# An order for all five engines worked out before emission, and five places for rows of weights

## The chip, the core and the metric

The kernel runs on one core of one Trainium2 chip. The metric is the device time of one execution in microseconds (us). PE is the matrix engine, DVE the vector engine, ACT the scalar engine, POOL the GpSimd engine, SP the engine whose queue issues most of the DMA transfers. All arithmetic is float32.

## What is computed

```python
# x: (8, 512, 256); Wg, Wu: (8, 256, 1024); Wd: (8, 1024, 256); Sg, Su, Sd: the shared expert's
g = einsum('bsd,edf->ebsf', x, Wg)
u = einsum('bsd,edf->ebsf', x, Wu)
expert_outs = einsum('ebsf,efd->ebsd', silu(g) * u, Wd)
expert_output = einsum('be,ebsd->bsd', gating_probs, expert_outs)
shared = einsum('bsf,fd->bsd', silu(x @ Sg) * (x @ Su), Sd)
out = x + (1 - sg) * expert_output + sg * shared
```

## The kernel before

The eight batch elements are two groups of four, and there are nine experts (the shared one is the ninth). A pair of group and expert is a **unit**; the 18 units run one after the other, named `0_0` to `1_8`. In a unit the four batch elements are combined with four **rows** of weights, a row being 256 columns of gate and up weights (two halves s, gate and up m). By sums and differences of inputs and of weights, prepared on POOL, DVE and ACT, products of several batch elements and rows share matmuls, so that there are fewer of them than in the plain product, and more element-wise work.

A unit is a sequence of 20 **items** (`SEQ`): hubs `h0` to `h3`, one per row (`P_step`, L338, and `Q_step`, L347), and 16 batches. A batch needs a weight difference `u` (`u_form`, L193, POOL), two more differences `w` (`w_form`: ACT multiplies, L203 and L207, then POOL, L210 and L212) and input tiles `v` and `b` that SP loads (L238, L244). In PSUM, ACT copies a sum `Pt` of a hub into a bank (`seed`, L265) and DVE subtracts another (L266); then PE multiplies by `u` and `v` (`R1`, L271), DVE opens a second bank (L281), PE multiplies by `w` and `b` (`R2`, L271), ACT takes silu (L285) and DVE forms the features `h` (L290). The items of the next unit's h0, 0s, h1 and 1s stand between the last batches of a unit (with ' in `SEQ`).

The down product runs along with this, one unit behind: chains `ch` (L454) with weights `ud`, `wd` (`d_forms`, L157 to L164, POOL), and `p`, `q` (L483) on `sums`, to which POOL adds features (L408, or a DMA with accumulation issued by POOL, L418). Partial results `V` go to memory and come back a unit later (L405, L394).

Counted in the code, a unit has 200 matmuls of 256 columns and 52 of 512. PE and POOL keep the order in which the code emits (`manual_schedule`); DVE, ACT and SP get theirs from the Tile scheduler.

The rows of weights lie in `raw`, which has room for four. `load_raw` (L126, four DMAs of 128 KB for a row) overwrites row r with the next unit's row r. It is emitted when the last batch that reads the old row has been formed two items ahead: row 0 with `03b`, row 1 with `13b`, rows 2 and 3 with `23b`. Then `make_at` changes a loaded row in place: ACT multiplies into `at` (L132), and POOL adds (L135). It is emitted two items ahead of its hub. `u` has two places and `w` three.

## Time and profile before

| | us |
|---|---|
| median of 2 runs | 2881.68 (2876.83 to 2886.54) |
| the profiled execution | 2880.3 |
| its span, first to last instruction | 2878.5 |
| PE busy | 2532.1 (88%) |
| DVE, POOL, ACT busy | 2102.2, 2040.5, 1236.2 |
| mean granted clock of PE | 0.947 |

The span is the profiled execution from its first to its last instruction; 1.8 us of the time lie outside it. In a timeline row the columns are start, duration, engine, line, operation, output and inputs, shape, and in brackets the idle time before it and what ended it. The mean of one instruction includes the time in which it overlaps the next one of its engine.

### The profile page before, as it was taken

Reading aid. Unit: us, or ns where it says so; the run is one execution under the profiler, and the core shown is the slowest. Engines: PE = TensorE matmul, PEld = TensorE weight load, DVE = VectorE, ACT = ScalarE, POOL = GpSimd, SP = SyncE. Lnnn points to the kernel's source line nnn. Section 1 sums busy time; section 2 is a strip of 40 time slices with the busy share of each in tenths; the row PEclk is TensorE's granted clock in tenths of the full one; section 3 lists DMA queues with packets and bytes.
Section 4 is the critical chain, followed back from the end, with each engine's and each line's share of the span. In section 5 each row is a group of like instructions: output and inputs, shape, how many; then the busy total and the mean of one; then the engine's idle time right before and its main releaser. Section 6 shows DMA issues by size and latency. Waiting matters only on the chain.

```text
span 2878.5 us, 30400 instructions
## 1 busy us (share of the span) xinstructions
PE 2532.1 (88%) x9112; PEld 1786.0 (62%) x9112; DVE 2102.2 (73%) x3006; ACT 1236.2 (43%) x2586; POOL 2040.5 (71%) x1676
## 2 busy tenths in 40 slices
PE   7789897898888798898987998989899888989897
PEld 5556565565556566666665666656666666666664
DVE  7877786788877676776776666768787676767677
ACT  5444343343434343444434444434344444444442
POOL 6968676685866678595948676767869585959683
PEclk8999998999989999999999999999999999999999
DMA  4476857658665756656465646565755657575646
GB/s 156 125 182 166 231 170 217 190 160 227 195 196 157 196 162 180 173 159 176 134 172 156 180 144 184 154 178 148 191 164 164 182 153 183 154 183 168 172 131 127
DMA packets 325633, 492.28 MB, mean 171 GB/s; under 512 B 73568, under 2 KB 204128, under 8 KB 325472
## 3 DMA queue, kind: packets, MB, share of 16 engines
q1 hardware_dynamic: 295808, 377.05, 41.5%
q0 software_dynamic: 29376, 113.25, 20.8%
q8 instruction: 75, 1.23, 0.2%
q14 instruction: 86, 0.70, 0.1%
q10 hardware_dynamic: 288, 0.04, 0.0%
HBM read 321.43 MB, written 55.57 MB: 131 GB/s over the span
## 4 chain that ended last, share of the span: by engine, by line
PE 47%; POOL 25%; issue 9%; DMA 8%; DVE 6%; ACT 2%; SPq 2%; POOLq 0%; ACTq 0%; DVEq 0%
PE ch L454 11%; POOL sums L408 7%; DMA raw<-in_L_cond_Wu_dram 5%; PE c_23b L271 3%; PE cd L338 3%; PE cd L347 3%; PE c_01a L271 3%; PE c_01b L271 3%; PE c_13b L271 3%; PE p L483 3%; PE c_13a L271 2%; PE q L483 2%; PE c_23a L271 2%; PE c_02b L271 2%; POOL wd L163 2%
## 5 line engine op out<-in xcount | busy, mean ns | idle before, releaser
L454 PE MATMUL ch<-X,ud 128*128 128x512 f32 x432 | 243.4, 648 | 0.0
L408 POOL TENSOR_TENSOR sums<-sums,h_03a 128x1024 f32<-128x1024 f32 x72 | 178.4, 2482 | 72.6 <-DVE h_03a L290 67.0
L193 POOL TENSOR_TENSOR u_01a<-raw 128x512 f32<-128x512 f32 x18 | 23.1, 1282 | 283.8 <-PE c_23b L271 280.8
L132 ACT ACTIVATE at<-raw 128x256 f32<-128x256 f32 x126 | 50.1, 412 | 394.5 <-DMA raw<-in_L_cond_Wu_dram 319.1
L338 PE MATMUL cd<-x,raw 128*128 128x256 f32 x576 | 158.4, 399 | 42.2 <-ACT sg_03b L285 35.1
L408 POOL TENSOR_TENSOR sums<-sums,h_02a 128x1024 f32<-128x1024 f32 x72 | 174.4, 2434 | 5.7 <-DVE h_02a L290 5.7
L347 PEld LDWEIGHTS cd<-x,raw 128*128 128x128 f32 x576 | 117.6, 205 | 91.9 <-issue 72.3
L408 POOL TENSOR_TENSOR sums<-sums,h_01a 128x1024 f32<-128x1024 f32 x72 | 171.3, 2379 | 1.4
L338 PEld LDWEIGHTS cd<-x,raw 128*128 128x128 f32 x576 | 111.5, 198 | 95.9 <-ACT sg_03b L285 48.1
L193 POOL TENSOR_TENSOR u_02b<-raw 128x512 f32<-128x512 f32 x18 | 23.3, 1295 | 206.9 <-PE c_02a L271 206.9
L347 PE MATMUL cd<-x,raw 128*128 128x256 f32 x576 | 157.6, 399 | 7.5 <-ACT Pt L342 7.5
L483 PE MATMUL p<-sums,rawd 128*128 128x512 f32 x288 | 147.9, 597 | 6.8 <-ACT p L480 6.8
L483 PE MATMUL q<-sums,rawd 128*128 128x512 f32 x288 | 148.6, 600 | 3.9 <-DVE accB L374 2.4
L266 DVE TENSOR_TENSOR c_23b<-c_23b,Pt 128x512 f32<-128x512 f32 x36 | 25.1, 698 | 155.2 <-ACT c_23b L265 154.5
L356 ACT COPY Dt<-cd 128x512 f32<-128x512 f32 x144 | 84.0, 584 | 105.7 <-DVE sums L290 104.9
L271 PE MATMUL c_23b<-v_23b,u_23b 128*128 128x256 f32 x144 | 53.7, 510 | 78.1 <-issue 73.4
L342 ACT COPY Pt<-cd 128x512 f32<-128x512 f32 x144 | 83.9, 583 | 65.9 <-PE cd L338 65.8
L271 PE MATMUL c_03b<-v_03b,u_03b 128*128 128x256 f32 x144 | 45.3, 441 | 69.7 <-DVE c_03b L266 43.5
L135 POOL TENSOR_TENSOR raw<-raw,at 128x256 f32<-128x256 f32 (+1 forms) x72 | 97.4, 1353 | 12.9 <-ACT at L132 12.9
L454 PEld LDWEIGHTS ch<-X,ud 128*128 128x128 f32 x432 | 89.4, 207 | 16.0 <-issue 1.9
L376 DVE TENSOR_TENSOR accB<-accB,ch 128x512 f32<-128x512 f32 x104 | 70.8, 681 | 31.8 <-PE ch L454 31.2
L374 DVE TENSOR_TENSOR accB<-ch,accB 128x512 f32<-128x512 f32 x116 | 79.2, 684 | 19.6 <-PE ch L454 19.5
(426 smaller groups left out, 8049.6 us busy)
## 6 DMA issues: line engine op xcount, KB each, us to landing
sums<-h_12a POOLq DMA_DIRECT2D x36, 1024.0 KB, 11.2
sums<-h_13a POOLq DMA_DIRECT2D x36, 1024.0 KB, 10.9
sums<-h_23a POOLq DMA_DIRECT2D x36, 1024.0 KB, 10.5
x<-xd SPq DMA_DIRECT2D x64, 512.0 KB, 3.8
Vd<-V SPq DMA_DIRECT2D x96, 256.0 KB, 2.0
V<-Vd SPq DMA_DIRECT2D x96, 256.0 KB, 3.1
raw<-in_L_cond_Wg_dram SPq DMA_DIRECT2D x128, 128.0 KB, 6.6
raw<-in_L_cond_Wu_dram SPq DMA_DIRECT2D x128, 128.0 KB, 5.7
```

What stands on the lines that cost most here:

```text
L135: gp.tensor_tensor(A, A, tmp[:, s0:], ALU.add)
L163: gp.tensor_tensor(W[:, 0], U, a[0], ALU.subtract)
L271: pe.matmul(half(bank, n), *one, start=False, stop=True, skip_group_check=True)
L338: pe.matmul(half(bank, s), raw[:, 2 * r + s, m, 0], half(hub.x[:, 0], s), start=s == 0, stop=True, skip_group_check=True,)
L342: ac.copy(Pt[:, m, 2 * r : 2 * r + 2], two(bank))
L347: pe.matmul(half(bank, s), raw[:, 2 * r + s, m, 1], half(hub.x[:, 1], s), start=False, stop=True, skip_group_check=True,)
L356: ac.copy(Dt[:, m, 2 * r : 2 * r + 2], two(bank))
L374: ve.tensor_add(acc[key], bank, acc[key])
L376: ve.tensor_sub(acc[key], acc[key], bank)
L408: gp.tensor_tensor(to, a, b, ALU.add)
L454: pe.matmul(two(bank), w[:, g], u.X[key, g] if what == "t" else group(t, g), start=what == "r" and g == 0, stop=True, skip_group_check=True,)
L483: pe.matmul(two(bank), rawd[:, i, g, 0 if what == "p" else 1], group(sums[:, at], g), start=not full and g == 0, stop=True, skip_group_che ...
```

## The change

The kernel's calls no longer go to the engines. They go to an `Engine` wrapper, which notes in a `Plan` what each call writes and reads and a price for it. When everything is noted, `Plan.order` walks through all calls with five clocks, one per engine. It takes again and again the call that could start first; among calls of one engine that could start at once, the one with the least `slack`, which is counted back from PE's calls in emitted order. Transfers have prices of their own, and the plan lets certain DVE and POOL instructions on SBUF (`lock`) not run at the same time. The calls are then made in this order, and all five engines keep it. A tile's place is given out as a ring, in the order of the tiles.

`raw` has five places instead of four. Row 0 of a unit is loaded with `23b` of the unit before the last, row 1 with `03b`, row 2 with `13b`, row 3 with `23b` of the last; `make_at` is noted one item ahead of its hub. A store of `V` is noted five ticks later. The identity and a small table of gates lie in space that `Dt` takes over later.

```diff
+    def order(self):
+        self.slacks()
...
+        while len(done) < len(self.ops):
+            best = None
+            for e in engines:
...
+                for op in waiting[e]:
+                    t = max(op.ready, free[e])
...
+                if could:
+                    first = min(c[0] for c in could)
+                    found = min(
+                        (c for c in could if c[0] <= first + (1300.0 if c[1] else 1.0)),
+                        key=lambda c: (c[2].slack + 2 * (c[0] - first), c[2].n),
+                    )
+                if found is not None and (best is None or found[0] < best[0]):
+                    best = found
...
+    def _note(self, what, call, out, writes, reads, kw):
+        e = self._name
+        if what == "dma_start":
...
+        n = out.size()
+        if e == "PE":
+            if what == "transpose":
+                return self._plan.add(e, 275.0, 110.0, call, writes, reads)
+            n = 1.6667 * n
+            return self._plan.add(e, n + 165.0, n + 5.0, call, writes, reads)
+        psum = any(v.buf.psum for v in (*writes, *reads))
+        a, b, c = self.PSUM[e] if psum else self.SBUF[e]
+        took = a + b * n
+        lock = not psum and what not in ("transpose", "memset") and (e == "POOL" or len(reads) > 1)
+        return self._plan.add(e, took, took - c, call, writes, reads, lock)
...
+    NR = 5
...
-    raw = const.tile([P, 8, 2, 2, P], F32, name="raw")
+    raw = const.tile([P, 2 * NR, 2, 2, P], F32, name="raw")
...
+    def slot(u, r, s=0):
+        return 2 * ((NI * u.n + r) % NR) + s
+
     def load_raw(u, r):
         for m in range(2):
             w = weights(u.e)[m].rearrange("(k p) (s r f) -> r s p k f", p=P, s=2, f=P)
             for s in range(2):
-                sp.dma_start(raw[:, 2 * r + s, m], w[r, s])
+                sp.dma_start(raw[:, slot(u, r, s), m], w[r, s])
...
+        if k + 1 < len(items) and items[k + 1].kind == "h":
+            make_at(items[k + 1].u, items[k + 1].r)
         if k + 2 < len(items):
             nxt = items[k + 2]
             if nxt.kind == "h":
-                make_at(nxt.u, nxt.r)
                 x_hub(nxt)
             else:
                 u_form(nxt)
                 w_form(nxt)
                 x_v(nxt)
-                for key, r in (("03b", 0), ("13b", 1), ("23b", 2), ("23b", 3)):
-                    if nxt.name == key and nxt.u.n + 1 < len(units):
-                        load_raw(units[nxt.u.n + 1], r)
         if k + 1 < len(items):
             nxt = items[k + 1]
             if nxt.kind != "h":
                 x_b(nxt)
+                for key, n, r in (("03b", 1, 1), ("13b", 1, 2), ("23b", 1, 3), ("23b", 2, 0)):
+                    if nxt.name == key and nxt.u.n + n < len(units):
+                        load_raw(units[nxt.u.n + n], r)
...
-    by_hand.close()
+    T = mybir.EngineType
+    with tc.manual_schedule(engines={T.PE, T.Pool, T.DVE, T.Activation, T.SP}):
+        for op in plan.order():
+            op.call()
```

**POOL at batch 02b of unit 1_2.** `u1_2_02b` needs the `u` place of `02a`, which is free when PE has used it. Before:

```order
L193 TENSOR_TENSOR u1_2_2s_11227<-raw_95 128x256
L210 TENSOR_TENSOR w1_2_2s_11229<-u1_2_2s_11227,w1_2_2s_11229 128x256
L212 TENSOR_TENSOR w1_2_2s_11229<-w1_2_2s_11229,u1_2_2s_11227 128x256
L193 TENSOR_TENSOR u1_2_02b_11262<-raw_95 128x512
L210 TENSOR_TENSOR w1_2_02b_11264<-u1_2_02b_11262,w1_2_02b_11264 128x512
L212 TENSOR_TENSOR w1_2_02b_11264<-w1_2_02b_11264,u1_2_02b_11262 128x512
L408 TENSOR_TENSOR sums_99<-sums_99,h0_1_2_01a_11174 128x1024
L150 TENSOR_TENSOR rawd_96<-rawd_96 128x2x128
L157 TENSOR_TENSOR ud1_2_01_11304<-rawd_96 128x256
L163 TENSOR_TENSOR wd1_2_01_11305<-ud1_2_01_11304,rawd_96 128x256
L164 TENSOR_TENSOR wd1_2_01_11305<-rawd_96,ud1_2_01_11304 128x256
L408 TENSOR_TENSOR sums_99<-sums_99,h1_1_2_01a_11179 128x1024
```

After, at the same place (every call now stands on the wrapper's line L337):

```order
L337 TENSOR_TENSOR u1_2_2s_11187<-raw_107 128x256
L337 TENSOR_TENSOR w1_2_2s_11204<-u1_2_2s_11187,w1_2_2s_11204 128x256
L337 TENSOR_TENSOR w1_2_2s_11204<-w1_2_2s_11204,u1_2_2s_11187 128x256
L337 TENSOR_TENSOR sums_101<-sums_101,h0_1_2_01a_11198 128x1024
L337 TENSOR_TENSOR sums_101<-sums_101,h1_1_2_01a_11215 128x1024 x2
L337 TENSOR_TENSOR u1_2_02b_11307<-raw_107 128x512
L337 TENSOR_TENSOR rawd_160<-rawd_160 128x2x128
L337 TENSOR_TENSOR u1_2_12a_11323<-raw_107 128x512
```

Three of the four additions of `01a` have moved from behind `u` of `02b` to ahead of it.

**ACT at batch 23b of unit 1_2.** `at1_3_2` and `at1_3_3` are rows 2 and 3 of the next unit, `c1_1_2_23b_0` and `_1` the seeds of 23b. Before:

```order
L342 COPY Pt_97<-cd_1_3_1_0_11904 128x512
L132 ACTIVATE at1_3_2_12067<-raw_95 128x256 x2
L285 ACTIVATE sg1_2_23a0_11911<-c0_1_2_23a_0_11863 128x512
L265 COPY c1_1_2_23b_0_11913<-Pt_97 128x512
L342 COPY Pt_97<-cd_1_3_1_1_11929 128x512
L285 ACTIVATE sg1_2_23a1_11927<-c1_1_2_23a_0_11820 128x512
L265 COPY c1_1_2_23b_1_11938<-Pt_97 128x512
```

After:

```order
L337 COPY Pt_208<-cd_1_3_1_0_11935 128x512
L337 ACTIVATE sg1_2_23a0_11949<-c0_1_2_23a_0_11903 128x512
L337 COPY c1_1_2_23b_0_11952<-Pt_208 128x512
L337 COPY Pt_208<-cd_1_3_1_1_11958 128x512
L337 ACTIVATE sg1_2_23a1_11964<-c1_1_2_23a_0_11825 128x512
L337 ACTIVATE at1_3_3_11968<-raw_107 128x256 x2
L337 COPY c1_1_2_23b_1_11977<-Pt_208 128x512
```

Row 2 is no longer ahead of the first seed (it stands 24 and 26 rows ahead of it, at 13b), and row 3, which stood 12 rows behind the second seed, is now right ahead of it.

SP's queue at the same place; each `raw` row is one transfer or several alike. Before:

```order
L238 DMA v1_2_23b_11894<-xs1_23b_5884 128x512
L244 DMA b1_2_23a_11859<-xs1_23a_5565 128x1024
L126 DMA raw_95<-in_L0_cond_Wg_dram 128x2x128 x2
L126 DMA raw_95<-in_L0_cond_Wu_dram 128x2x128 x2
L126 DMA raw_95<-in_L0_cond_Wg_dram 128x2x128 x2
L126 DMA raw_95<-in_L0_cond_Wu_dram 128x2x128 x2
L238 DMA v1_3_1s_11957<-xs1_1s_6411 128x256
L244 DMA b1_2_23b_11959<-xs1_23b_5884 128x1024
```

After:

```order
L337 DMA v1_2_23b_11866<-xs1_23b_5458 128x512
L337 DMA b1_2_23a_11881<-xs1_23a_5265 128x1024
L337 DMA raw_107<-in_L0_cond_Wg_dram 128x2x128
L337 DMA raw_107<-in_L0_cond_Wu_dram 128x2x128
L337 DMA raw_107<-in_L0_cond_Wg_dram 128x2x128 x3
L337 DMA raw_107<-in_L0_cond_Wu_dram 128x2x128 x3
L337 DMA v1_3_1s_11919<-xs1_1s_5844 128x256
L337 DMA b1_2_23b_11930<-xs1_23b_5458 128x1024
```

There are eight row transfers here in both, before for rows 2 and 3 of the next unit, in this order; after, three for row 0 of the unit after next, then the four of row 3, then the last of row 0.

**DVE at batch 01b of unit 1_3.** `X230` and `X231` are the two differences for the chain of batch pair 23 of unit 1_2, `c1_1_3_01b_0` is a seed of 01b. Before:

```order
L387 TENSOR_TENSOR X230_1_2_12094<-h1_1_2_23a_11944,h0_1_2_23a_11936 128x512
L290 SCALAR_TENSOR_TENSOR sums_99<-sg1_3_1s0_12043,coef_100,c0_1_3_1s_1_12009 128x256
L281 TENSOR_TENSOR c0_1_3_01a_1_12056<-Dt_98,c1_1_3_01a_1_12014 128x512
L387 TENSOR_TENSOR X231_1_2_12096<-h1_1_2_23a_11944,h0_1_2_23a_11936 128x512
L266 TENSOR_TENSOR c1_1_3_01b_0_12046<-c1_1_3_01b_0_12046,Pt_97 128x512
```

After:

```order
L337 SCALAR_TENSOR_TENSOR sums_101<-sg1_3_1s0_12075,coef_127,c0_1_3_1s_1_12039 128x256
L337 TENSOR_TENSOR X230_1_2_12081<-h1_1_2_23a_11989,h0_1_2_23a_11971 128x512
L337 TENSOR_TENSOR c0_1_3_01a_1_12087<-Dt_96,c1_1_3_01a_1_12049 128x512
L337 TENSOR_TENSOR c1_1_3_01b_0_12085<-c1_1_3_01b_0_12085,Pt_208 128x512
L337 TENSOR_TENSOR V13_1_2_11835<-V13_1_2_11835,ch13_1_2_11926 128x512
```

The second difference, which stood right ahead of the seed, now stands eight rows behind it.

PE's own order hardly changes: of the instructions whose names can be matched, 98 in 100 stand within five places of where they stood.

## Rows read from the trace of the kernel before

**Rows 1.** The page: the span, and each engine's busy time with its share of the span and its instructions.
```profile
span 2878.5 us, 30400 instructions
PE 2532.1 (88%) x9112; PEld 1786.0 (62%) x9112; DVE 2102.2 (73%) x3006; ACT 1236.2 (43%) x2586; POOL 2040.5 (71%) x1676
```

**Rows 2.** Stretches of the span: length, busy time of PE, PEld (weight loads), DVE, ACT and POOL with their counts, then PE's granted clock, the DMA engines' busy share and GB/s.
```profile
250.00:1015.00 765.00, 661.14 (x2323) 460.47 (x2323) 578.11 (x824) 316.82 (x671) 528.23 (x424) 0.93 0.69 193
1168.00:2712.00 1544.00, 1386.63 (x5050) 986.57 (x5049) 1099.55 (x1584) 677.08 (x1407) 1113.87 (x911) 0.95 0.61 166
```

**Rows 3.** The chain of work that ended last, whole run: start, duration, what. The two are the same wait, ahead of batch 23b, five units apart.
```profile
1777.76 5.07 issue
...
2543.43 5.30 issue
```

**Rows 4.** The same chain in a stretch in which PE waited for nothing: start, duration, what, records (a matmul is two records).
```profile
1909.45 0.86 PE ch L454 x2
...
1916.34 0.86 PE ch L454 x2
```

**Rows 5.** What PE waited for, from 1168 to 2712 us: engine, what it was to do, whom it waited for, total us, times, longest. These are the five largest.
```profile
PE c_23b L271 <- issue: 45.6, 9, 5.3
PE c_03b L271 <- DVE c_03b L266: 25.6, 9, 4.4
PE c_01b L271 <- POOL wd L163: 23.9, 9, 2.7
PE c_03b L271 <- POOL u_03b L193: 18.0, 9, 2.2
PE cd L338 <- ACT sg_03b L285: 17.7, 9, 3.8
```

**Rows 6.** PE's granted clock (behind POOL's count) in three short stretches of unit 1_2, each behind a wait of PE; columns as in rows 2.
```profile
1882.70:1886.10 3.40, 3.40 (x16) 2.61 (x15) 2.99 (x5) 2.31 (x6) 2.72 (x5) 1.00 1.05 239
1936.00:1940.00 4.00, 3.98 (x8) 2.52 (x9) 3.95 (x7) 2.78 (x5) 0.00 (x0) 0.50 0.09 32
1956.40:1959.80 3.40, 3.40 (x8) 2.06 (x9) 2.25 (x4) 1.56 (x3) 3.32 (x4) 0.59 1.03 204
```

**Rows 7.** Timeline of unit 1_2 on ACT and, in the middle, DVE: batch 03b (first two) and batch 23b.
```profile
1877.32 0.42 ACT L132 ACTIVATE at<-raw 128x256 f32<-128x256 f32 x1 [7.62 <-DMA raw<-in_L_cond_Wu_dram]
1878.05 0.48 DVE L290 SCALAR_TENSOR_TENSOR sums<-sg_3s,coef,c_3s 128x256 f32<-128x256 f32 x1 [6.42 <-ACT sg_3s L285]
...
1916.44 0.42 ACT L207 ACTIVATE w_23b<-raw 128x256 f32<-128x256 f32 x1 [1.20 <-PE c_13b L271]
1927.82 0.42 ACT L132 ACTIVATE at<-raw 128x256 f32<-128x256 f32 x1 [3.96 <-DMA raw<-in_L_cond_Wu_dram]
1933.66 0.42 ACT L132 ACTIVATE at<-raw 128x256 f32<-128x256 f32 x1 [5.43 <-DMA raw<-in_L_cond_Wu_dram]
1934.60 0.59 ACT L265 COPY c_23b<-Pt 128x512 f32<-128x512 f32 x1
```

**Rows 8.** Timeline of SP's queue in the same place, start and time of issue: the first and the last pair of the eight row loads; then ACT's wait for row loads in the whole run (total us, times, longest).
```profile
1919.71 1.87 SPq L126 DMA_DIRECT2D raw<-in_L_cond_Wg_dram  x2
...
1925.79 2.55 SPq L126 DMA_DIRECT2D raw<-in_L_cond_Wu_dram  x2
ACT at L132 <- DMA raw<-in_L_cond_Wu_dram: 319.1, 52, 10.5
```

**Rows 9.** Timeline of unit 1_2 on POOL and PE, batches 02b and 03b.
```profile
1825.62 1.28 POOL L193 TENSOR_TENSOR u_02b<-raw 128x512 f32<-128x512 f32 x1 [11.00 <-PE c_02a L271]
...
1872.23 1.26 POOL L193 TENSOR_TENSOR u_03b<-raw 128x512 f32<-128x512 f32 x1
1873.55 1.13 PE L271 MATMUL c_03b<-v_03b,u_03b 128*128 128x256 f32 x4 [2.16 <-POOL u_03b L193]
```

**Rows 10.** POOL's groups by form, whole run: count, busy us, mean ns of one, idle before and releaser. Additions to `sums`, then one form each of 128x512 and 128x256.
```profile
L408 POOL TENSOR_TENSOR sums<-sums,h_01a 128x1024 f32<-128x1024 f32 x72 | 171.3, 2379 | 1.4
L193 POOL TENSOR_TENSOR u_12a<-raw 128x512 f32<-128x512 f32 x18 | 23.5, 1306 | 0.0
L193 POOL TENSOR_TENSOR u_02b<-raw 128x512 f32<-128x512 f32 x18 | 23.3, 1295 | 206.9 <-PE c_02a L271 206.9
L164 POOL TENSOR_TENSOR wd<-rawd,ud 128x256 f32<-128x256 f32 x54 | 40.5, 750 | 0.0
```

**Rows 11.** DVE's L387, a difference of two tiles in SBUF: durations in ns, shortest, median and longest; then two of them and the seed of 01b behind them in unit 1_2's timeline, and PE's wait there.
```profile
L387 DVE TENSOR_TENSOR X<-h_03a x36: 691/2063/2850, 139.8 to 2809.6; 128x512 f32<-128x512 f32 x36
1950.90 1.65 DVE L387 TENSOR_TENSOR X<-h_23a 128x512 f32<-128x512 f32 x1
1953.46 2.21 DVE L387 TENSOR_TENSOR X<-h_23a 128x512 f32<-128x512 f32 x1
1955.59 0.68 DVE L266 TENSOR_TENSOR c_01b<-c_01b,Pt 128x512 f32<-128x512 f32 x1
1956.38 1.41 PE L271 MATMUL c_01b<-v_01b,u_01b 128*128 128x256 f32 x4 [2.66 <-POOL wd L163]
```

**Rows 12.** The first matmul of unit 0_0 and the last of the run.
```profile
9.97 1.22 PE L338 MATMUL cd<-x,raw 128*128 128x256 f32 x2 [0.52 <-DMA raw<-in_L_cond_Wg_dram]
...
2868.92 1.98 PE L483 MATMUL q<-sums,rawd 128*128 128x512 f32 x4 [0.73 <-ACT accb L490]
```

More of the change, by code (lines that the diff above doesn't have):

```diff
@@ L14, with __init__, real @@
 PSUM = bass.MemoryType.PSUM
+class Buf:
+    def __init__(self, plan, pool, shape, dtype, name, tag=None, bufs=None, psum=False):
+        self.plan, self.pool, self.args = plan, pool, (shape, dtype)
+        self.kw = {"name": name, **({"tag": tag} if tag else {}), **({"bufs": bufs} if bufs else {})}
+        self.psum, self.name = psum, name
+        self.ring = None
+        if tag is not None and bufs:
+            self.ring = plan.rings.setdefault((id(pool), tag), Ring(bufs))
+        self.last, self.readers, self.ops = {}, {}, []
+        self.number = None
+        self.tile = None
+        n = 1
+        for k in shape[1:]:
+            n *= k
+        if psum:
+            at = np.zeros(n, np.int32)
+        else:
+            at = np.arange(n, dtype=np.int32) // 128
+        parts = 1 if psum else 4
+        at = at[None] + np.arange(parts, dtype=np.int32)[:, None] * (n // 128 + 1)
+        self.shadow = at.reshape([parts, *shape[1:]])
+    def real(self):
+        if self.tile is None:
+            self.tile = self.pool.tile(*self.args, **self.kw)
+        return self.tile
@@ new lines, with __init__, tile, __getattr__ @@
+class PlannedPool:
+    def __init__(self, plan, pool, psum, bufs):
+        self.plan, self.pool, self.psum, self.bufs = plan, pool, psum, bufs
+    def tile(self, shape, dtype, name, tag=None, bufs=None):
+        n = bufs or self.bufs
+        buf = Buf(self.plan, self.pool, list(shape), dtype, name, tag, n if tag else None, self.psum)
+        return View(buf, buf.shadow, [])
+class Engine:
+    PSUM = {"DVE": (160.0, 1.03, 83.0), "ACT": (164.0, 0.836, 94.0)}
+    SBUF = {"DVE": (141.0, 1.043, 83.0), "ACT": (191.0, 0.848, 94.0), "POOL": (186.0, 2.12, 44.0)}
+    def __init__(self, plan, name, real):
+        self._plan, self._name, self._real = plan, name, real
+    def __getattr__(self, what):
+        def called(*a, **kw):
+            views = [x for x in (*a, *kw.values()) if isinstance(x, View)]
+            out = a[0]
+            writes = [out] if isinstance(out, View) else []
+            reads = [v for v in views if v is not out]
+            def call():
+                r = [x.real() if isinstance(x, View) else x for x in a]
+                k = {n: x.real() if isinstance(x, View) else x for n, x in kw.items()}
+                return getattr(self._real, what)(*r, **k)
+            return self._note(what, call, out, writes, reads, kw)
+        return called
+    def _note(self, what, call, out, writes, reads, kw):
+        e = self._name
+        if what == "dma_start":
+            v = writes[0] if writes else reads[0]
+            run = min([kw.pop("run", 4096), *(x.run() for x in (*writes, *reads))])
+            size = v.size() * 512 * v.shadow.shape[0] / v.buf.shadow.shape[0]
+            run = max(32, min(4096, run))
+            one = {4096: 159.0, 2048: 84.0, 1024: 46.0, 512: 27.0}.get(run, max(9.0, run * 0.042))
+            heavy = "accum_op" in kw
+            if heavy:
+                one *= 2.06
+            work = size / run / 16 * one
+            hold = 1190.0 if e == "POOL" else 320.0 if run >= 1024 else 580.0
+            share = one / (one + 328.0)
+            return self._plan.add(e, 2500.0 + work, hold, call, writes, reads, False, (work, e == "POOL", share))
+        n = out.size()
[9 more added lines that the diff above has]
+        return self._plan.add(e, took, took - c, call, writes, reads, lock)
@@ L32 @@
     nc = tc.nc
-    gp, ve, ac, pe, sp = nc.gpsimd, nc.vector, nc.scalar, nc.tensor, nc.sync
+    plan = Plan()
+    gp, ve, ac, pe, sp = (
+        Engine(plan, name, real)
+        for name, real in (
+            ("POOL", nc.gpsimd), ("DVE", nc.vector), ("ACT", nc.scalar), ("PE", nc.tensor), ("SP", nc.sync)
+        )
+    )
     B, S, D = x.shape
@@ L819 @@
             load_raw(units[0], r)
+    load_raw(units[1], 0)
     make_coef()
```

246 lines of the change are left out of this document (232 added, 14 removed).

## The prediction

> **What bounds the kernel now.** I read the busy shares first [rows 1]: PE is busy for 88% of the span, DVE for 73%, POOL for 71%. So the question is what fills PE's time beyond its matmuls. For the price of a matmul I took a stretch of the chain in which PE waits for nothing [rows 4]: from 1909.45 to 1916.34 us stand eight slots, a slot being one matmul of 512 columns or two of 256, so a slot is 6.89 / 8 = 0.861 us. A unit has 52 matmuls of 512 and 200 of 256, hence 152 slots or 130.9 us. The same wait returns after five units 765.67 us later [rows 3], so a unit takes 153.1 us. The 22.2 us between are to be explained. PE's waits of 1168 to 2712 us [rows 5] name five places that return in every unit; their sum of 130.8 us over nine units is 14.5 us a unit. The granted clock there is 0.95 [rows 2], and 5% of 153.1 us is 7.7 us. 130.9 + 14.5 + 7.7 = 153.1: the unit is accounted for, and it is PE's waits and the clock that they cost, 0.53 us of clock for each us of wait.
>
> Outside of 18 such units lie 2878.5 - 2755.8 = 122.7 us. 10.0 us pass before the first matmul and 9.6 after the start of the last [rows 12]; the other 103 us are the units that differ, above all those in which the second group's inputs are made ready (clock 0.93, DMA share 0.69 [rows 2]).
>
> **What the change does, place by place.** The same instructions are issued, so the 130.9 us stay. PE's order hardly moves. What moves is the work that PE waits for.
>
> *Batch 03b, 2.8 us a unit behind DVE (25.6 / 9).* ACT, in order, stood 7.62 us at the product for row 0 of the next unit; behind it stood a silu for which DVE then idled 6.42 us, and a seed [rows 7]. With the fifth place row 0 is loaded with the last unit's 23b, some 100 us earlier. This wait goes, all of it.
>
> *The next unit's h0, 2.0 us (17.7 / 9), behind ACT's silu of 03b.* Ahead of that silu stood the product for row 1. Row 1 is now loaded one step earlier, with 03b. Counted in PE's order from the matmul that lets ACT read the old row for the last time to the first matmul behind the product, it had 10 slots (8.6 us); now it has 16 (13.8 us), and row 2 has 20 (17.2 us) at 13b. The wait should go.
>
> *Batch 23b, 5.1 us (45.6 / 9), named "issue".* In unit 1_2 ACT stood twice at row 2 until 1933.66, and only then copied the seed that PE needed [rows 7]. In the new order that product stands far ahead, at 13b. But row 3, which had until 01b, is now right ahead of the second seed. The price: the old rows were last read from 1916.44, and the four transfers of row 2 had landed at 1933.66 [rows 7], 17.2 us later; SP needed 8.6 us to issue all eight transfers (1919.71 to 1928.34), 1.1 each [rows 8]. Row 3 is now fourth to seventh of eight, so 3.2 us later, 20.4. POOL takes u of 23b ahead of other work, and the loads can start when ACT has read (4 x 0.4 after 1916.44) rather than at 1919.71: 1.7 us off, 18.7. The order gives 20 slots, 17.2 us, less 2.3 for two products, the copy and DVE's subtraction, so 14.9. That is 3.8 us late. If the transfers are as quick as row 2's were and start earlier, it is 0.6; if all eight have to land, 5. I take 3.5, close to the middle, with 0 and 6 as ends.
>
> *Batch 03b, 2.0 us (18.0 / 9), behind POOL's u.* POOL waited 11.00 us for the place of u_02b and from 1825.62 worked without pause until u_03b was done at 1873.49, 47.9 us [rows 9]. PE has 53 slots between (45.6 us), so PE is 2.3 us late; it waited 2.16. In the old order eight additions to sums, 14 instructions of 128x512 and 14 of 128x256 stand in this string; in the new one five, eleven and 14. Three additions of 2.38 and three others of 1.30 [rows 10] make 11.0 us less. The additions went into the idle time ahead of u_02b, of which there are 206.9 us in the run [rows 10]. u_03b is ready some 8.7 us ahead of PE: the wait goes.
>
> *Batch 01b, 2.7 us (23.9 / 9), put down to POOL's wd.* DVE's seed of 01b began at 1955.59, behind two differences of 1.65 and 2.21 us, and PE went on at 1956.38 [rows 11]. Now one difference stands behind the seed, and POOL's wd ahead of its other work. That takes off about 2.2 us. The rest, and its likes where seeds are tight, I put at 0.6 us. The difference lasts 0.69 us at best and 2.06 at the median [rows 11], so DVE is held up by something. [...]
>
> *Everything else:* small waits that a fixed order of five engines makes where a price is off by some tenths, 0.4 us a unit (0 to 3). Later stores of V cost nothing: the value is wanted a unit later.
>
> **The sum.** New waits: 3.5 + 0.6 + 0.4 = 4.5 us a unit, with clock 4.5 x 1.53 = 6.9. A unit is 137.8 us, 18 are 2480. Of the 122.7 us outside, the 20 at the ends stay, and I halve the 103, since part is what the five places cost in those units and part is the inputs' own traffic: 51. Span 2480 + 20 + 51 = 2551, time 2553 us, against 2880.3 for the profiled execution, which the median of 2881.68 hardly differs from: 11% less.
>
> Does a wait that short cost clock? Behind a wait of 2.66 us the clock is 0.59, behind 23b's of some 5 us it is 0.50, but behind one of 2.16 us it is 1.00 [rows 3, 6, 9, 11]. [...]
>
> **Rivals.**
>
> *The order fits (2430).* Row 3 lands in time, and 1.0 us a unit is left: 18 x 132.4 = 2383, with 20 + 26 outside and 2. For it: no string of POOL in the new order is tighter than PE's time. Against it: row 2's 17.2 us.
>
> *The wait for rows only moves (2760).* Rows 1 and 2 are late too (1 and 2 us), row 3 by 6.2, with the 1.0 of before 10.2, with clock 15.6: 18 x 146.5 = 2637, and 123 + 2. For it: a list that starts everything as early as its prices allow puts ACT in front of a transfer that is just due, and ACT's queue holds seeds and silus behind it.
>
> *POOL keeps its idle time (2880).* POOL is busy 1113.87 of 1544 us, 110.5 a unit [rows 2]; if its waits for u places stay as they are and only change their neighbours, its unit stays 153 us. Against it: the additions did move into one of these waits.
>
> *Slower (about 3350).* In a fixed order nothing passes a late row on ACT. If it waits at 03b, 13b and 23b as long as at worst before, 10.5 us [rows 8], PE loses 31.5, with clock 48.2 a unit: 18 x 179.1 + 125. It decides as soon as new waits pass 14.5 us a unit, where the old ones lie. Against it: rows 0 to 2 all have more slots than before.
>
> **How the numbers follow.** My forecast 0.60; the order fits 0.13; the wait moves 0.16; no gain 0.07; slower 0.04. The range 2435 to 2760 reaches from the first rival to the second, leaves out the last two and the edges, and holds row 3's bounds (0 and 6 us are 2457 and 2622). 2% is about what a measurement of this kernel can tell from no change. Faster by more: 0.60 + 0.13 + 0.14 (the worst of the wait that moves is not) = 0.87; within 2%: 0.08; slower: 0.05.
>
> **What would show it.** In the profile after: units of about 138 us; PE's busy share at 93% or more; no wait of ACT for a row at 03b and 13b; one at 23b, ahead of the second seed, of some us; PE's waits for c_03b and for the hub gone; POOL's wait for u_02b far below 206.9 us; granted clock near 0.97. I am wrong if ACT's wait for rows stays near 319 us, or if small waits of PE, each below 1 us, come to more than 3 us a unit.

## The result, and the profile after

The changed kernel takes 2683.95 us, median of 2 runs (2679.48 to 2688.43), against 2881.68 before: a ratio of 0.931, 95% interval 0.922 to 0.941. The forecast was 2553 with a range of 2435 to 2760. It is faster, and by 198 us where 329 were expected. The experiments below look for the other 131 us.

The page of the changed kernel, to be read beside [rows 1], and its steady stretch beside [rows 2], with the same columns:

```profile
span 2677.6 us, 30533 instructions
PE 2458.2 (92%) x9112; PEld 1745.9 (65%) x9112; DVE 2158.8 (81%) x3006; ACT 1232.7 (46%) x2585; POOL 2021.1 (75%) x1676
```

```profile
1280.00:2490.00 1210.00, 1127.33 (x4177) 805.79 (x4178) 961.40 (x1319) 561.87 (x1171) 914.89 (x759) 0.97 0.65 176
```

PE is busier and the clock is up from 0.947 to 0.975, as it should be. But DVE, which has the same 3006 instructions, is busy 2158.8 us instead of 2102.2. That is the first hint: some of its work has become longer.

What PE waits for between 1168 and 2550 us, the answer to [rows 5]:

```profile
PE c_03b L337 <- issue: 30.8, 6, 5.2
PE c_13b L337 <- issue: 19.4, 6, 3.3
PE c_23b L337 <- DVE c_23b L337: 10.5, 6, 2.2
PE c_0s L337 <- issue: 6.1, 5, 1.3
PE c_01b L337 <- DMA b_01b<-xs_01b: 5.2, 6, 1.8
```

All five places of before are gone from their form: no wait for POOL's u of 03b, none for its wd at 01b, none for ACT's silu of 03b ahead of the hub. In their place stand waits at 03b and 13b that the profile names "issue". They come in some units and not in others. Measured from the first matmul of 02a to the next, units 0_6, 1_0, 1_3 and 1_4 take 133.3, 143.6, 138.4 and 135.7 us, while seven others between 0_7 and 1_7 take 146.6 to 149.3, 148.3 on the mean. The four average 137.7 us, near the 137.8 of the forecast, but they spread from 133.3 to 143.6, so that is no confirmation. The seven are 10.5 us longer.

One of the long ones, first POOL and then DVE, ACT and PE around batch 03b of unit 1_1:

```profile
1564.30 1.27 POOL L337 TENSOR_TENSOR w_03b<-u_03b,w_03b 128x512 f32<-128x512 f32 x1
1565.52 1.27 POOL L337 TENSOR_TENSOR w_03b<-w_03b,u_03b 128x512 f32<-128x512 f32 x1
...
1569.87 1.27 POOL L337 TENSOR_TENSOR w_13a<-raw,u_13a 128x512 f32<-128x512 f32 x1
1575.29 0.73 POOL L337 TENSOR_TENSOR raw<-raw,at 128x256 f32<-128x256 f32 x1 [4.14 <-ACT at L337]
```

```profile
1564.35 0.74 DVE L337 SCALAR_TENSOR_TENSOR h_12a<-sg_12b,coef,c_12b 128x512 f32<-128x512 f32 x1
1565.12 6.57 DVE L337 TENSOR_TENSOR X<-h_12a 128x512 f32<-128x512 f32 x1
1571.62 0.47 DVE L337 SCALAR_TENSOR_TENSOR sums<-sg_3s,coef,c_3s 128x256 f32<-128x256 f32 x1
...
1572.12 0.59 ACT L337 COPY c_03b<-Pt 128x512 f32<-128x512 f32 x1 [6.17 <-DVE sums L337]
1573.99 2.05 PE L337 MATMUL c_03b<-v_03b,u_03b 128*128 128x256 f32 x4 [5.19 <-issue]
```

DVE's difference X, 0.69 us at best, lasts 6.57. It begins under a POOL instruction and ends 0.55 us after the last instruction of POOL's run, which ends at 1571.14. Behind it wait a feature, ACT's copy for the seed of 03b (6.17 us) and PE (5.19 us). No wait in the profile names X: DVE counts as busy, and PE's wait is called "issue".

The same chain behind an X of 03a gives the 3.2 us at 13b. POOL, DVE and PE in the same unit:

```profile
1589.80 1.18 POOL L337 DMA_DIRECT2D sums<-h_12a  x1
...
1598.63 2.72 POOL L337 TENSOR_TENSOR sums<-sums,h_03a 128x1024 f32<-128x1024 f32 x1
1593.25 8.66 DVE L337 TENSOR_TENSOR X<-h_03a 128x512 f32<-128x512 f32 x1
1603.82 1.10 PE L337 MATMUL c_13b<-v_13b,u_13b 128*128 128x256 f32 x4 [3.24 <-issue]
```

The two differ in what POOL does ahead of X. In seven units an X of 12a begins 22 us into a run of POOL without a DMA. In the same seven an X of 03a begins 8.5 us into a run, 3.4 us behind a DMA that POOL issues in it.

The other X, by batch pair (shortest, median, longest in ns), beside [rows 11]:

```profile
L337 DVE TENSOR_TENSOR X<-h_12a x36: 682/1186/6940, 104.7 to 2600.4; 128x512 f32<-128x512 f32 x36
L337 DVE TENSOR_TENSOR X<-h_03a x36: 677/1548/12306, 131.4 to 2621.4; 128x512 f32<-128x512 f32 x36
```

Before, the longest of all was 3.02 us. The sum over 216 X is 362.5 us, against 296.0 before.

### The profile page after: what moved, and what is told of

It reads as the page before. It is cut to its first block, busy times and chain, and to the rows that moved or that the text cites. A ratio compares the mean times of both kernels' runs of the same rounds, so it can differ in the third digit from the quotient of the medians.

```text
span 2677.6 us, 30533 instructions
## 1 busy us (share of the span) xinstructions
PE 2458.2 (92%) x9112; PEld 1745.9 (65%) x9112; DVE 2158.8 (81%) x3006; ACT 1232.7 (46%) x2585; POOL 2021.1 (75%) x1676
## 4 chain that ended last, share of the span: by engine, by line
PE 62%; DMA 13%; DVE 9%; POOL 8%; issue 5%; ACT 2%; SPq 1%; POOLq 0%; ACTq 0%; DVEq 0%
PE ch L337 13%; PE cd L337 6%; PE q L337 4%; DMA raw<-in_L_cond_Wu_dram 3%; PE p L337 3%; PE c_12a L337 3%; PE c_12b L337 3%; PE c_23b L337 3%; PE c_02a L337 3%; DMA b_01b<-xs_01b 3%; PE c_02b L337 3%; PE c_13b L337 3%; PE c_01b L337 3%; PE c_03b L337 3%; PE c_03a L337 3%
## 5 line engine op out<-in xcount | busy, mean ns | idle before, releaser
L337 PE MATMUL cd<-x,raw 128*128 128x256 f32 x1152 | 301.6, 385 | 14.3 <-DVE x L337 6.2
L337 PEld LDWEIGHTS cd<-x,raw 128*128 128x128 f32 x1152 | 219.5, 192 | 138.3 <-issue 84.4
L337 POOL TENSOR_TENSOR sums<-sums,h_01a 128x1024 f32<-128x1024 f32 x72 | 175.8, 2463 | 103.0 <-DVE h_01a L337 102.9
L337 PE MATMUL ch<-X,ud 128*128 128x512 f32 x432 | 225.1, 604 | 3.5 <-DVE X L337 2.5
L337 POOL TENSOR_TENSOR raw<-raw,at 128x256 f32<-128x256 f32 (+1 forms) x72 | 88.7, 1232 | 136.8 <-ACT at L337 127.9
L337 POOL TENSOR_TENSOR sums<-sums,h_03a 128x1024 f32<-128x1024 f32 x72 | 184.9, 2618 | 2.1 <-DVE h_03a L337 2.1
L337 POOL TENSOR_TENSOR sums<-sums,h_02a 128x1024 f32<-128x1024 f32 x72 | 171.4, 2393 | 3.5 <-DVE h_02a L337 3.5
L337 PE MATMUL p<-sums,rawd 128*128 128x512 f32 x288 | 147.5, 597 | 4.3 <-ACT p L337 4.0
L337 PE MATMUL q<-sums,rawd 128*128 128x512 f32 x288 | 147.6, 596 | 1.7 <-ACT accb L337 1.7
L337 ACT COPY Pt<-cd 128x512 f32<-128x512 f32 x144 | 84.1, 584 | 110.5 <-PE cd L337 110.1
L337 ACT COPY Dt<-cd 128x512 f32<-128x512 f32 x144 | 83.9, 583 | 75.0 <-DVE sums L337 67.9
L337 DVE TENSOR_TENSOR X<-h_03a 128x512 f32<-128x512 f32 x36 | 113.9, 3199 | 0.5
L337 DVE TENSOR_TENSOR accB<-ch,accB 128x512 f32<-128x512 f32 x116 | 79.1, 683 | 28.6 <-PE ch L337 28.0
L337 PEld LDWEIGHTS ch<-X,ud 128*128 128x128 f32 x432 | 83.0, 193 | 20.7 <-DVE X L337 5.4
L337 POOL TENSOR_TENSOR ud<-rawd 128x256 f32<-128x256 f32 x108 | 89.4, 828 | 1.5 <-PE ch L337 0.7
L337 PE MATMUL c_03b<-v_03b,u_03b 128*128 128x256 f32 x144 | 45.7, 447 | 47.9 <-issue 42.9
L337 DVE TENSOR_TENSOR accB<-accB,ch 128x512 f32<-128x512 f32 x104 | 70.6, 678 | 22.1 <-PE ch L337 22.1
L337 PE MATMUL c_01a<-b_01a,w_01a 128*128 128x256 f32 x288 | 74.4, 398 | 13.8 <-DMA b_01a<-xs_01a 7.4
L337 DVE TENSOR_TENSOR X<-h_12a 128x512 f32<-128x512 f32 x36 | 84.8, 2358 | 1.7 <-PE ch L337 1.3
L337 ACT ACTIVATE at<-raw 128x256 f32<-128x256 f32 x126 | 49.0, 411 | 79.7 <-DMA raw<-in_L_cond_Wu_dram 60.0
L337 PEld LDWEIGHTS c_01a<-b_01a,w_01a 128*128 128x128 f32 x288 | 56.4, 198 | 37.2 <-issue 17.1
L337 PE MATMUL c_23b<-b_23b,w_23b 128*128 128x256 f32 x288 | 73.7, 389 | 7.2 <-DMA b_23b<-xs_23b 7.2
```

The lines of the kernel that those rows point to most:

```text
L337: return getattr(self._real, what)(*r, **k)
```

## The experiments

Two theories stood against each other. **Theory 1:** POOL keeps DVE out of a difference of two SBUF tiles as long as POOL works without a pause, and the list's order gives POOL such stretches. **Theory 2:** the seeds are late for another reason (rows, transfers), and X only fills the time. All medians below are of four runs, where no other number is given; the kernel before took 2875 to 2885 beside them.

**x_one.** X with one SBUF input in place of two; the order is word for word that of the changed kernel.

```diff
-            ve.tensor_sub(X, group(u.h_[key, 1], g), group(u.h_[key, 0], g))
+            one = group(u.h_[key, 1], g)
+            op = ve.tensor_sub(X, one, group(u.h_[key, 0], g))
+            op.call = partial(
+                lambda X, one: nc.vector.transpose(
+                    X.real().rearrange("p a b -> p (a b)"), one.real().rearrange("p a b -> p (a b)")
+                ), X, one
+            )
```

> The changed kernel, every call in the same place, but DVE's difference X of two SBUF tiles is a transposition of one of them (128x512, 0.70 us where the changed kernel uses that form); so the second features are left out of the down product's middle term. Theory 1 (DVE's difference is held up for as long as POOL works without a pause, 6.5 and 8.7 us in seven of ten units, and the seeds of 03b and 13b stand behind it): every X takes 0.7 us, PE's waits at 03b (5.1), 13b (3.2) and 0s (1.3) go, the units of 148 us come to about 136, and the time to 2590 (2570 to 2620). Theory 2 (the seeds are late because of ACT's row of weights or of transfers, and X only fills a time in which DVE waits anyway): within 1% of 2684.

2559.01 us (2546.23 to 2567.77), ratio to before 0.888 (0.884 to 0.891), faster than the range given for theory 1. Every X lasts 0.7 us (150.8 in sum), the waits "issue" at 03b, 13b and 0s are gone, and the eleven units from 0_6 to 1_7 take 135.7 us on the mean instead of 144.5. Theory 2 falls.

**pool_yields.** Nothing is left out; POOL waits for X. (SYNC stands for a dependency; in this run's trace POOL then waits for DVE's X, 27.7 us in sum ahead of additions to `sums` alone.) Where two X stand in the list with no POOL instruction between them, one wait serves both: built from the list there are 175 waits for the 216 X, not 216 as expected.

```diff
+            op = ve.tensor_sub(X, group(u.h_[key, 1], g), group(u.h_[key, 0], g))
+            op.yields = True
...
+        last = None
         for op in plan.order():
-            op.call()
+            made = op.call()
+            if op.yields:
+                last = made
+            elif last is not None and op.engine == "POOL" and op.lock:
+                tc.add_manual_dep(made.ins, last.ins.name, SYNC, reason="yield")
+                last = None
```

> The changed kernel with one more wait: the POOL instruction that the plan puts behind a difference X waits until X is done (216 waits); nothing is left out. Theory 1: no X lasts longer than what is left of one POOL instruction and 0.6 us, 3 us at most; the waits at 03b and 13b go; POOL loses some 0.2 us at each wait, 2.4 us of a unit in which it has over 20 idle; 2610 (2580 to 2650). Theory 2: 2684, or slower by what POOL loses, up to 2730.

2551.47 us (2551.09 to 2552.22), ratio to before 0.886 (0.884 to 0.889). So 175 more waits make the changed kernel 5% faster, and faster than the range given for theory 1. With row3_first below, it is the fastest version of this study. Its page, then X of the same two pairs:

```profile
PE 2421.3 (95%) x9112; PEld 1733.6 (68%) x9112; DVE 2015.7 (79%) x3006; ACT 1233.6 (48%) x2585; POOL 1969.5 (77%) x1676
```

```profile
L338 DVE TENSOR_TENSOR X<-h_12a x36: 677/968/2946, 96.3 to 2472.9; 128x512 f32<-128x512 f32 x36
L338 DVE TENSOR_TENSOR X<-h_03a x36: 676/692/1794, 122.2 to 2493.9; 128x512 f32<-128x512 f32 x36
```

The eleven units take 134.95 us, of which PE waits 2.6. POOL waits 88 us for X in its nine largest groups of such waits, but it is busy 52 us less than in the changed kernel.

**two_yield.** As pool_yields, but only for X of pairs 12 and 03 (72 X, for which the list makes 55 waits).

```diff
+            op.yields = key in ("12", "03")
```

> The changed kernel in which POOL waits only for the differences X of batch pairs 12 and 03 (72 waits instead of the 216 of pool_yields). If the long differences of these two (6.5 and 8.7 us in seven units, 12.3 in another) are the cause of what the changed kernel loses, it is as fast as pool_yields: 2551 (2540 to 2575). If the others, of 1 to 3 us, count as well, some of the 132 us stay: 2600 or more.

2559.82 us (2555.32 to 2561.55). 55 waits bring 124 of the 132 us: the X of these two pairs are the cause, and the others cost little.

**order_alone** and **places_alone** take the change apart.

```diff
# order_alone, against the changed kernel
-    NR = 5
+    NR = 4
...
-                for key, n, r in (("03b", 1, 1), ("13b", 1, 2), ("23b", 1, 3), ("23b", 2, 0)):
+                for key, r in (("03b", 0), ("13b", 1), ("23b", 2), ("23b", 3)):
```

In order_alone rows are loaded and changed two items ahead again, as before. places_alone, against the kernel before:

```diff
+    NR = 5
...
+                for key, n, r in (("03b", 1, 1), ("13b", 1, 2), ("23b", 1, 3), ("23b", 2, 0)):
```

> The changed kernel with four places for rows, loaded and changed where the kernel before did it; only the order from the list is left of the change. By the prediction's terms the fifth place is worth the rows' part, 2.8 + 2.0 + 5.1 - 3.5 = 6.4 us of waits a unit, with clock 9.8, 176 us in all: 2860, and ACT's wait for rows is near 319 us again. Rival (the list puts other work around a late row, and the order does nearly all): 2700 or less.

> The kernel before with five places, the rows loaded and changed where the changed kernel does it, and its own scheduling. By the prediction's terms: 2882 - 176 = 2706, with PE's waits for ACT's silu of 03b and at 23b largely gone and those for POOL's u of 03b and wd at 01b left. Rival (the order does nearly all): 2840 or more.

order_alone: 2651.71 us (2636.04 to 2659.13), ratio to before 0.920 (0.917 to 0.924). With a place fewer it is 32 us faster than the changed kernel. places_alone: 2698.80 us (2689.05 to 2699.92), 0.937 (0.934 to 0.940): 181 us gained where 176 were worked out. What ACT waits for rows in order_alone, and what POOL waits for u of 02b in places_alone:

```profile
ACT at L337 <- DMA raw<-in_L_cond_Wu_dram: 96.8, 36, 6.1
```

```profile
POOL u_02b L199 <- PE c_02a L277: 218.6, 18, 19.9
PE c_03b L277 <- DVE c_03b L287: 21.5, 9, 2.7
```

With four places the list's order leaves 97 of the 319 us that ACT waited for rows [rows 8]: it puts other work ahead of a late row, which the prediction had not priced. With five places and the old scheduling POOL's idle time stays (206.9 before), and at 03b a wait of 2.4 us a unit for DVE takes the place of the old one. One of them, on ACT, DVE and PE:

```profile
1629.96 0.42 ACT L136 ACTIVATE at<-raw 128x256 f32<-128x256 f32 x1 [6.64 <-POOL rawd L154]
1630.29 0.58 ACT L291 ACTIVATE sg_03a<-c_03a 128x512 f32<-128x512 f32 x1
1630.90 0.70 DVE L287 TENSOR_TENSOR c_03b<-Dt,c_03b 128x512 f32<-128x512 f32 x1 [3.99 <-ACT sg_03a L291]
1631.65 1.94 PE L277 MATMUL c_03b<-b_03b,w_03b 128*128 128x256 f32 x4 [2.69 <-DVE c_03b L287]
```

ACT again stands at a row's product ahead of a silu; it no longer waits for the row but, by the profile, for POOL. So the 181 us are not the terms of the 176: at 23b the wait is gone where 3.5 us a unit were to stay, and at 03b one has come back.

**order_yields.** order_alone with the waits of pool_yields.

> order_alone (four places) with the 216 waits of POOL for X, so that the two parts can be told apart without the long differences. By the prediction's terms the fifth place is worth 9.8 us a unit: 2551 + 176 = 2727, no better than order_alone. If the order does most of what both do: order_alone's 2652 less what X costs it (its X last 290 us in sum, pool_yields' 201): 2600, and the fifth place is worth some 50 us.

2600.33 us (2596.14 to 2602.76). With X out of the way the parts can be told: the order with these waits is worth 280 us, of which X itself can be up to 58 (x_one_before below), and the fifth place 49 more. In the changed kernel the fifth place cost 32 us instead, because the order that goes with it happens to be worse for X. X of 12a begins 22 us into a run of POOL in both; it lasts 3.4 us in order_alone, where POOL pauses 2.8 us after it began, and 6.5 in the changed kernel. X of 03a lasts 2.9 us at most in all but one unit of order_alone, and 8.7 in seven of the changed kernel.

**row3_first.** pool_yields with row 0 of the unit after next loaded at another place.

```diff
-                for key, n, r in (("03b", 1, 1), ("13b", 1, 2), ("23b", 1, 3), ("23b", 2, 0)):
+                for key, n, r in (("02a", 1, 0), ("03b", 1, 1), ("13b", 1, 2), ("23b", 1, 3)):
...
```

> pool_yields with row 0 of the unit after next loaded with 02a of the next unit instead of with 23b, so that row 3's four transfers have SP's queue to themselves at 23b. If row 3 is what holds 23b (the term of 3.5 us a unit), ACT's wait for rows falls below 15 us, and the 1 to 3 us that PE still waits at 23b go: 2530 (2520 to 2545). If what is left there is the traffic of the inputs b, no change: 2551 within 0.5%.

2550.33 us (2545.31 to 2554.81), no change. ACT's wait for these rows is 30.4 us in the run, and it was 30.7 in pool_yields, so the other place did not bring row 3 sooner, and the run is no test of its price. What PE waits at 23b is mostly the transfer of b (7.5 us over nine units in pool_yields, 7.8 here). In one unit of each, row 3 is still 5 us late, and PE waits 3.0 and 3.9 us there.

**x_one_before.** The kernel before with the X of x_one.

> The kernel before with X as in x_one (a transposition, one input). Its X last 296 us in sum, 150 would be left. By the prediction, which put a part of the wait at 01b (2.7 us a unit) on two of them, and 03b's wait behind a row: 1 to 2 us a unit, 25 to 55 us, 2825 to 2855. If X costs the kernel before nothing that other waits don't cover: 2880 within 0.5%.

2822.44 us (2812.26 to 2827.13), 0.979 (0.976 to 0.982). X cost the kernel before 58 us. The wait at 01b put down to POOL's wd, 33.9 us in the kernel before, is gone from PE's list. At the chain, PE's waits for the same instruction are up from 2.2 us to this:

```profile
PE ch L456 <- POOL wd L163: 12.5, 17, 1.1
```

So most of the 33.9 us was DVE's X, and some 10 us may have been POOL.

**pe_pool_kept.** The list keeps PE and POOL alone.

```diff
-    with tc.manual_schedule(engines={T.PE, T.Pool, T.DVE, T.Activation, T.SP}):
+    with tc.manual_schedule(engines={T.PE, T.Pool}):
```

> The changed kernel, but only PE and POOL keep the list's order; DVE, ACT and SP are ordered by the Tile scheduler, as in the kernel before, from calls made in the list's order. If what counts is POOL's order and the fifth place, as the prediction's terms have it (the rows, POOL's string ahead of u_03b, its wd ahead of 01b), it is as fast as the changed kernel, or faster where its DVE falls behind other POOL work than in the long differences: 2600 to 2690. If the order of DVE and ACT around late rows counts, ACT's wait for rows rises above 150 us and the time to 2750 or more.

2817.56 us (2814.97 to 2820.45). The time is that of the second expectation, its sign only in part: ACT waits 111.7 us for those rows, not 150, but in the wrong place.

```profile
1684.55 0.42 ACT L337 ACTIVATE at<-raw 128x256 f32<-128x256 f32 x1 [8.13 <-DMA raw<-in_L_cond_Wu_dram]
1684.87 0.58 ACT L337 ACTIVATE sg_03b<-c_03b 128x512 f32<-128x512 f32 x1
```

A row stands again ahead of the silu of 03b, as in [rows 7]; X of 12a lasts 6.5 us here too, in seven units, and 7.2 in one. PE's waits between 1168 and 2670 us:

```profile
PE cd L337 <- DVE sums L337: 53.3, 7, 9.6
PE c_03b L337 <- issue: 28.1, 6, 4.7
PE cd L337 <- ACT sg_03b L337: 27.0, 7, 4.4
```

The third is the row ahead of the silu of 03b. The first, in the unit of 1725 us, is of the same kind: ACT stood 5.78 and 5.20 us at products of rows, until 1723.80, ahead of a silu for which DVE and then the hub waited. The second is X. So rows behind which ACT's order leaves silus cost more than X here, and the list's order for POOL without the others' gives only 2%, places included.

**lock_probe** measures the dispute by itself: POOL differences without a pause, and X beside them.

> Not the model at all (its output is zeros): 16 short runs of nine POOL differences of 128x512 without a pause, beside DVE's differences X of two tiles in SBUF (128x512), four to a run, with one to four instructions that read PSUM ahead of each, so that X meets POOL's instructions at different phases. Kinds of run: A, POOL's instructions depend on nothing; B, every second one on the one ahead of it; C, as A behind a DMA issued by POOL; D, as A with waits on POOL's own semaphore that are long met. If DVE takes turns with POOL, every X lasts what is left of POOL's instruction and 0.55 us, 1.8 us at most, in all four. If POOL keeps DVE out as long as its next instruction starts before the last one ends, X lasts to the end of the run (5 to 10 us) in C, and in A and D where X begins late in an instruction, but not in B, where each second instruction can start only when the one ahead is done.

In kinds A, B and D every X lasts 0.7 to 1.8 us: DVE takes its turn behind POOL's current instruction, and the next POOL instruction lasts 1.7 us instead of 1.26. In kind C an X that begins under an instruction behind the DMA lasts until POOL's run is over; one that began at 128.15, 0.66 us ahead of the first instruction behind the DMA, was still let in (0.68 us). X of one run of kind A, then the first two runs of kind C:

```profile
9.87 1.72 DVE L54 TENSOR_TENSOR X<-da,db 128x512 f32<-128x512 f32 x1
12.85 1.64 DVE L54 TENSOR_TENSOR X<-da,db 128x512 f32<-128x512 f32 x1
...
130.08 9.33 DVE L54 TENSOR_TENSOR X<-da,db 128x512 f32<-128x512 f32 x1
...
148.11 10.46 DVE L54 TENSOR_TENSOR X<-da,db 128x512 f32<-128x512 f32 x1
```

A DMA issued by POOL is enough: the instructions behind it start 0.3 us before the one ahead has ended (0.04 in kinds A and D), and DVE isn't let in. That is what X of 03a meets in the changed kernel. But X of 12a has no such DMA ahead of it, and theory 1 as worded is too wide: in A and D POOL works for 12 us without a pause, and DVE gets its turns.

**lock_probe2** tries the age of the run.

> As lock_probe (the output is zeros), three other kinds of run. E: 31 POOL differences of 128x512 without a pause and without a DMA (38 us), with an X every 5 to 6 us. F: the same run, with no X in the first 18 to 20 us and two after that. G: a DMA issued by POOL, three differences, one that waits for ACT (a pause), nine more, with two X behind the pause. In the traces of the kernels X was kept out in two cases: behind a DMA of POOL's, and late in a run (39 of 131 that began 16 to 25 us into a run without a DMA, 1 of 937 before). If the age of the run by itself does it, X is kept out in F (10 us or more) and takes turns in E until about 16 us; if an X that is let in resets it, never in E. If the age is only a companion of something else in the kernel, X lasts 1.8 us at most in E and F. G: if a pause ends the state that the DMA leaves, 1.8 us at most; if not, X lasts to the end of the run.

An X of kind E, then the two of a run of kind F and POOL's run beside them (30 instructions in one row):

```profile
29.38 1.67 DVE L53 TENSOR_TENSOR X<-da,db 128x512 f32<-128x512 f32 x1
```

```profile
118.40 16.09 DVE L53 TENSOR_TENSOR X<-da,db 128x512 f32<-128x512 f32 x1
136.46 0.68 DVE L53 TENSOR_TENSOR X<-da,db 128x512 f32<-128x512 f32 x1
...
97.25 36.69 POOL L47 TENSOR_TENSOR acc<-zero,b 128x512 f32<-128x512 f32 x30
```

In F an X that comes 22 us into the run waits for the rest of it, 16.09 us, and so it is in all four runs (13.9 to 16.1). In E, where one comes every 6 us, it is let in each time, until 29 us (1.67 us at 35.94, 22 us into the run): an X that got in starts the count anew. In G the pause, 0.73 us of idle time, ends what the DMA began: 0.7 to 1.7 us.

**pool_pauses.** Only pauses; nobody waits for DVE.

```diff
+        n, last = 0, None
...
+            made = op.call()
+            if op.engine == "POOL" and op.lock:
+                n += 1
+                if n % 3 == 0 and last is not None:
+                    tc.add_manual_dep(made.ins, last.name, SYNC, reason="pause")
+                last = made.ins
+            elif op.engine == "POOL":
+                last = None
```

> The changed kernel in which every third POOL instruction waits for the POOL instruction right ahead of it; nothing waits for DVE. In the kernel before such waits on POOL's own results leave a gap of 0.08 us, and no run of POOL without a gap is longer than 9.3 us; in the changed kernel 49 are longer than 16 us. If a gap of 0.08 us is what lets DVE in, no X lasts much above 3 us, PE's waits at 03b and 13b go, and the time is near that of pool_yields, plus what some 30 gaps of 0.12 us a unit cost POOL: 2560 (2545 to 2590). If DVE gets in only where POOL really waits for it, X stays at 6.5 and 8.7 us in several units and the time above 2640.

2567.19 us (2561.27 to 2575.8), ratio to before 0.890 (0.888 to 0.893). X of 12a is 2.90 us at most; ten of the 216 last over 2.9, the longest 5.2, all of them in runs in which POOL issued a DMA ahead of X. POOL's longest run is 12.7 us. So for the long runs theory 1 is shown from the other side: gaps of 0.08 us for POOL are enough.

## Why the prediction was right in part

*What bounds it, and the unit.* 130.9 us of matmuls, waits, and clock: this held. Without held-up differences (pool_yields) a unit is 134.95 us, 130.9 + 2.6 of waits + 1.4. In the eleven units of the changed kernel it is 130.9 + 9.0 + 4.6, so 0.5 us for each us of wait as assumed. But the clock is not all of that. Of the 4.6 it is at most 3.4, half of the 6.8 us a unit that stand at half speed; of pool_yields' 1.4 it is some 0.5, from three stretches of 3.4 us in eleven units. Some 1 us a unit is left in both, and what it is, these runs do not show. Short waits cost less clock than the 0.53 taken for each: some 0.5 us for the 2.6 in pool_yields.

*03b behind DVE and the hub behind ACT's silu.* Both waits went. But the reason given, the fifth place, is one of two: order_alone doesn't have them either. (In six of its units PE waits 2.0 us at 03b. The profile puts that down to POOL's change of a row, but it goes in order_yields, so it is X's.) The forecast put 176 us on the place; alone it brings 181, on top of the order 49.

*POOL's string ahead of u_03b.* It went as forecast: POOL's wait for the place of u_02b, 206.9 us [rows 10], is 2.3 us.

```profile
L337 POOL TENSOR_TENSOR u_02b<-raw 128x512 f32<-128x512 f32 x18 | 27.8, 1547 | 2.3 <-PE c_02a L337 2.2
```

*23b behind row 3.* Mechanism and place were right. Unit 1_1, ACT and PE:

```profile
1634.14 0.42 ACT L337 ACTIVATE at<-raw 128x256 f32<-128x256 f32 x1 [5.15 <-DMA raw<-in_L_cond_Wu_dram]
1634.46 0.58 ACT L337 COPY c_23b<-Pt 128x512 f32<-128x512 f32 x1
...
1635.92 1.46 PE L337 MATMUL c_23b<-v_23b,u_23b 128*128 128x256 f32 x4 [2.05 <-DVE c_23b L337]
```

The term was 3.5 us a unit, within 0 to 6; PE waits 2.05 where row 3 is late, and 10.5 us in more than nine units, 1.1 on the mean. Mis-sized by 2.4.

*01b.* Forecast 0.6 us, measured 5.2 over nine units, 0.6. The match is luck: the 0.6 was for seeds, and PE now waits there for the transfer of b. That the old wait was mostly X, as the prediction read it, x_one_before shows.

*"Everything else", 0.4 us a unit with ends of 0 and 3: this is the step that failed.* 30.8 + 19.4 + 6.1 = 56.3 us, 5.9 a unit, came from X. The prediction saw that X took 0.69 to 2.06 us and that something holds DVE up. That a POOL with less idle time could lengthen X was not priced, although the forecast itself counted on POOL's idle time going. The longest X of 03a in its rows, 2.85 us [rows 11], came from a POOL that pauses. Counted in the traces, with POOL's instructions and DMA issues as one run while no gap exceeds 20 ns: the kernel before has no run above 9.3 us, places_alone none above 9.3, the changed kernel 49 above 16 us, the longest 35.9. In the kernel before 453 gaps below 0.15 us break the runs, most of 0.08 where a POOL instruction reads what the one ahead has written ("without pause", as the prediction has it of 1825 to 1873 us, was wrong in that). The list's order puts other work between the two, and 69 are left. These gaps looked like a loss, and they were what let DVE in: with such gaps put back (pool_pauses) X of 12a lasts 2.90 us at most. A trace of the other cause already stood in the rows: the X of 2.21 us [rows 11] begins 0.3 us behind a DMA that POOL issues, and is kept out for one POOL instruction more than the one under which it begins.

*Outside of the units.* The prediction halved 103 us to 51. In the changed kernel 18 units of 144.45 are 2600 of 2677.6 us, so 77 lie outside, near the 71 forecast; but this rests on the units being long. With pool_yields 18 units of 134.95 are 2429 of 2549.1 us, so 120 us lie outside, and nothing is halved. The unit was 2.9 us too long, which is 51 us. So the 2553 of the forecast and the 2551 of pool_yields agree to 2 us by two errors of some 50 that cancel, and this agreement is no proof of the terms.

*The rivals.* "The order fits" went wrong over X; "the wait for rows only moves" too: ACT waits 60.0 us for these rows instead of 319. "POOL keeps its idle time" is refuted by the 2.3 us, and the slower case by the rows. The one that came true, a wait in a new place with 5.9 us a unit, was in none of them. Of the signs named, the clock (0.975), POOL's wait and the row at 23b came; units of 138 us and a busy share of 93% came only with X out of the way (pool_yields: 134.95 us, 95%).

*DVE's turns, and the clock.* In kinds A, B, D and E DVE got in behind POOL's current instruction (X lasts 1.8 us at most); in C and F it did not: DVE lost up to 7 and up to 12 times in a row (10.46 and 16.09 us). If it lost to one POOL instruction only, X would last at most some 2.35 + 0.55 us here, an estimate from POOL's addition of 128x1024 (2.35 us at 1543.03 in the changed kernel) and X's end behind POOL's instruction. As to the clock: in the units from 0_6 on of twelve kernels (all the runs but the two probes), all 67 waits of PE of 3.5 us or more had a stretch at half speed behind them, of 174 between 1.5 and 3.5 us 76 had one, and of 391 between 0.2 and 1.5 us 3. The stretches last 3.4 us or a multiple of it (in the kernels before and after 3.41, 6.83, 10.24 or 13.65 us, but for the last of each trace, which goes on past its end). So the long waits cost clock each time, those of 1.5 to 3.5 us in fewer than half of the cases, and the prediction's 0.53 is too much for the small waits of pool_yields. No sharp limit lies between 2.16 and 2.66 us, as the prediction's three waits might suggest: the stretch at clock 1.00 in [rows 6] stands behind a wait of 2.67 us (at 1879.93), the one at 0.59 behind 2.66.

## What to carry to other kernels

When a trace shows one engine held up by another's work, look at how long the other runs without a gap, not only at how busy it is. Here POOL's gaps below 0.15 us went from 453 to 69, and the longest X of 12a from 2.03 to 6.94 us; the profile books the held-up engine as busy (DVE 2158.8 us instead of 2102.2). If one instruction's longest duration is several times its shortest, find what bounds it before making its neighbour denser. A plan that prices a lock as turn-taking should also enforce the turns, by a real wait at the one or two places where it counts: here 55 waits were worth 124 us.
